# Turning x and y in pairs by VectorE's 32x32 blocks and block transfers, with wider FFN tiles, in an attention-and-FP4-FFN kernel

## The chip, the core and the metric

The kernel runs on one core of a Trainium2 chip. The metric is the device time of one execution in microseconds (us). Its engines are named as in the profile: PE is TensorE's matrix multiply and PEld its weight load, DVE is VectorE, ACT is ScalarE, POOL is GpSimd, and SP is the engine that issues most transfers (DMA).

## What is computed

The input x is 8 sequences of 1024 rows of 512 numbers, all float32. First comes attention with low-rank projections, then a feed-forward network (FFN) whose inputs and weights are rounded to a 4-bit floating-point grid; each has a layer norm before it and a residual sum after it.

```python
x = x + attn(layernorm(x))     # c_q = x@W_DQ, c_kv = x@W_DKV; 16 heads of 32 + 16 rotary;
                               # scores clipped to +-80, causal softmax, @V, @W_O
x = x + ffn(layernorm(x))

def fp4_linear(x, w): return quant(x) @ quant(w).T
def ffn(y): return fp4_linear(silu(fp4_linear(y, w_gate)) * fp4_linear(y, w_up), w_down)
# quant: blocks of 16 along the last axis; scale = max|.|/6; round to 0, .5, 1, 1.5, 2, 3, 4, 6
```

W_DQ and W_DKV are 512x128, the FFN's inner width is 1408 (11 chunks of 128).

## The kernel before

The 8192 rows are cut into 16 units of 512 rows (two per sequence), each of 4 tiles of 128 rows; two tiles are a pair, so there are 32 pairs. A matmul sums over the partitions of both operands, so the normed rows of x and the quantized rows of y (the input of FFN) must stand with their 512 columns on partitions. Both are turned by TensorE: four 128x128 transposes against an identity per tile into a PSUM bank, which ACT copies out. For x this is `turn` (L182 to L188), called by `rows_turned` (L361), and the result is the tile xnT. For y it is `turned` (L753 to L765), and the result is yT, two tiles of 512 columns per pair.

**Order of the work.** The streams of PE, DVE and ACT are written out by the program in the order of its calls. SP's transfers are placed by a scheduler, and each waits for what it needs; a place in the queue is not passed. Attention over a unit (`attention`, L667) goes step by step through 4 groups of heads and 3 or 7 key blocks; between its steps it runs `fillers`: pieces of the next unit's projection (`project_pieces`, L342), merged by their costs with pieces of FFN (`ffn_pieces`, L854) of rows that are already projected. In units 0 to 3 the pieces of the weights' preparation (`weight_pieces`, L270) stand where FFN's stand later. A small planner, `Clock`, holds expected times of PE, DVE and ACT. DVE work that is not due (all of `quantize` and the norms of y) waits in a list and is laid into DVE's stream where the planner expects room (`fill`), or at the latest where a piece asks for it by key (`need`).

**A unit's projection**: load of tiles xl, `norms`, `rows_turned`, then `rotation` (matmuls pr with wkr, pp with wdkv) and `rotated` (pp with wdq, pf), each for half a unit (one pair).

**FFN of pair m**: `fetch` loads y from mid in DRAM; `begin` lays norm and quantize; `turned`; `gate` (L786) and `up` (L805) for k = 0 to 5 run `hidden`, 16 matmuls (8 for k = 5) of 256 columns into a bank pg; ACT copies pg into h and takes its silu; DVE multiplies with the second pg (L813). Every two h tiles are quantized together, their blocks turned by DVE before and after (L214), in passes of 512 columns. `down` (L825) sums 11 chunks into pd, and `finish` adds the residual. The tiles yT, h and the raw weights share the pool `ring`: 9 places of 512 columns.

**Output projection**: at the third step of the next unit's attention `fetch_wo` (L707) loads W_O, 1 MB, into a place of the pool pT as soon as one is free, and `out_proj` (L711) runs four groups of matmuls po, adds x (reloaded as xo) and stores mid.

Of the kernel before, what the change touches and what calls it, by code (L numbers as in the profile page):

```python
# [42 lines left out]
def tile_mla_then_fp4_ffn(  # L43
# [23 lines left out]
    ring = ctx.enter_context(tc.tile_pool(name="ring", bufs=9))  # L67
# [42 lines left out]
    def mm(dst, par=1, **kw):  # L110
        shape = kw.get("tile_position", ()) and "rows" or dst.shape[0]
        clk.pe += 0.00168 * dst.shape[-1] / par + (0.1 if shape != clk.shape else 0.0)
        clk.shape = shape
        nc.tensor.matmul(dst, **kw)  # L114
# [19 lines left out]
    ones = const.tile([P, DH], F32, name="ones")  # L134
    nc.vector.memset(ones, 1.0)
    neg_half = const.tile([P, 1], F32, name="neg_half")
# [27 lines left out]
    xls = {(0, t): load_x(0, t, p2, ("xl", "y")[t // 2]) for t in range(NT)}  # L164
# [26 lines left out]
    def quantize(parts, key, turned=False):  # L191

        ends, at = [], 0
        for part in parts:
            ends.append((at, at + part.shape[1] // BLK))
            at = ends[-1][1]
        nb = at
        got = {}

        def amax(k):  # L200
            if k == 0:
                got["sc"] = p1.tile([P, 88], F32, tag="sc", name="sc")[:, :nb]
                got["rs"] = p1.tile([P, 88], F32, tag="rs", name="rs")[:, :nb]
            nc.vector.tensor_reduce(
                got["rs"][:, slice(*ends[k])],
                parts[k].rearrange("p (b k) -> p b k", k=BLK),
                AX.X,
                ALU.max,
                apply_absolute_value=True,
            )  # L210

        def turn_blocks(part):
            slack(
                0.06 + 0.0013 * part.shape[1], lambda: nc.vector.transpose(part, part), key  # L214
            )
# [11 lines left out]
        for k, part in enumerate(parts):  # L227
            if turned:
                turn_blocks(part)
            slack(0.06 + 0.0012 * part.shape[1], lambda k=k: amax(k), key)  # L230
        slack(1.1 + 0.008 * nb, scales, key)
        for part, end in zip(parts, ends):
            step, bl = part.shape[1], slice(*end)
            nbl = step // BLK
            part3 = part.rearrange("p (b k) -> p b k", k=BLK)

            def times(which, part3=part3, bl=bl, nbl=nbl):
                by = got[which][:, bl].unsqueeze(2).to_broadcast([P, nbl, BLK])
                if which == "sc":
                    nc.vector.tensor_tensor(part3, part3, by, ALU.mult)  # L240
                else:


                    nc.vector.scalar_tensor_tensor(
                        part3, part3, BELOW_ONE, by, ALU.mult, ALU.mult
                    )

            def steps(part=part, step=step):  # L250
                got["m"] = m = p1.tile([P, 512], F32, tag="m", name="m")[:, :step]
                nc.vector.tensor_scalar(
                    m.bitcast(U32), part.bitcast(U32), EXP_MASK, None, ALU.bitwise_and
                )
                nc.vector.tensor_scalar(m, m, 1.0, MAGIC, ALU.max, ALU.mult)

            def to_grid(op, part=part):
                nc.vector.tensor_tensor(part, part, got["m"], op)  # L258

            pass_cost = 0.06 + 0.00125 * step  # L260
            slack(pass_cost, lambda f=times: f("rs"), key)
            slack(1.2 * pass_cost, steps, key)
            slack(pass_cost, lambda f=to_grid: f(ALU.add), key)
            slack(pass_cost, lambda f=to_grid: f(ALU.subtract), key)
            slack(pass_cost, lambda f=times: f("sc"), key)
            if turned:
                turn_blocks(part)


    def weight_pieces():  # L270
# [10 lines left out]
        def load(i):  # L281

            raws[i] = []
            for src, _ in chunks[i]:
                for off in range(0, src.shape[1], 512):
                    width = min(512, src.shape[1] - off)
                    raw = ring.tile([P, 512], F32, tag="h", name="wraw")[:, :width]
                    nc.sync.dma_start(out=raw, in_=src[:, off : off + width])
                    raws[i].append(raw)
            quantize(raws[i], ("w", i))  # L290

        def piece(i, k, dst, off, n):
            clk.need(("w", i))
            turn(raws[i][k], dst[:, off : off + n], n)
            if k == len(raws[i]) - 1:
                raws.pop(i)
                if i + 3 < len(chunks):
                    load(i + 3)

        pieces = []  # L300
        for i, parts in enumerate(chunks):
            if len(parts) > 1:
# [5 lines left out]
        begun = [(0.5, lambda i=i: load(i)) for i in range(3)]  # L308
        return begun + [(0.5, lambda x=x: piece(*x)) for x in pieces]


    def normed(xt, key):
        got = {}

        def stats():
            pool, tag = (small, "nx") if key[0] == "x" else (p1, "ny")
            own = pool.tile([P, 10], F32, tag=tag, name=tag)
            st, ve = own[:, 0:6], own[:, 8:9]
            got["mv"], got["rstd"] = mv, rstd = own[:, 6:8], own[:, 9:10]
# [22 lines left out]
    def project_pieces(u):  # L342
# [3 lines left out]
        def fetch(*ts):  # L346
            for t in ts:
                if (u, t) not in xls:
                    xls[u, t] = load_x(u, t, p2, "xl")

        def norms(k, *ts):

            for t in ts:
                if k == 0:
                    state["norm", t] = normed(xls[u, t], ("x", u, t))
                cost, run, _ = state["norm", t][k]
                clk.dve += cost
                run()
                state["ready", t] = clk.dve

        def rows_turned(t):  # L361
            g, k = divmod(t, 2)
            if k == 0:
                state["xnT"] = p1.tile([P, NDC, 256], F32, tag="xnT", name=f"xnT_{u}_{g}")
            normed_at = state["ready", t]
            clk.pe = max(clk.pe, normed_at)
            turn(xls.pop((u, t)), state["xnT"][:, :, k * P : (k + 1) * P], NDC)

        def latent(g, w, dst):
            cols = slice(g * 256, (g + 1) * 256)  # L370
            pp = bank("pp")
            for i in range(NDC):
                mm(
                    pp[:, :256],
                    lhsT=w[:, i, :],
                    rhs=state["xnT"][:, i, :],
# [5 lines left out]
        def rotation(g):  # L382
            if g == 0:
# [3 lines left out]
                )  # L387
            pr = bank("pr")
            for i in range(NDC):
                mm(  # L390
                    pr[32 * i : 32 * i + 32, :256],
                    par=4,
                    lhsT=wkr[:, i, :],
                    rhs=state["xnT"][:, i, :],
# [29 lines left out]

        if u == 0:
# [3 lines left out]
            first, second = [], []  # L429
        else:  # L430
            first = [
                (1.0, lambda: fetch(0, 1)),
                (1.5, lambda: norms(0, 0, 1)),
                (3.0, lambda: norms(1, 0, 1)),
            ]
            second = [lambda k=k: norms(k, 2, 3) for k in range(2)]
        return [
            *first,
            (0.5, lambda: rows_turned(0)),
            (0.5, lambda: both(lambda: rows_turned(1), *[lambda: fetch(2, 3)] * (u > 0))),  # L440
            (2.3, lambda: both(lambda: rotation(0), *second[:1])),
            (2.2, lambda: both(lambda: rotated(0), *second[1:])),
            (2.0, lambda: None),
            (0.5, lambda: rows_turned(2)),
            (0.5, lambda: rows_turned(3)),
# [299 lines left out]
    def fetch(n):  # L745
        ys[n] = p2.tile([P, D], F32, tag="y", name=f"y_{n}")
        nc.sync.dma_start(out=ys[n], in_=mids[tiles[n]])

    def begin(n):
        begin_norms([(ys[n], ("y", n))])  # L750
        quantize([ys[n]], ("y", n))

    def turned(n):  # L753
        m, t = divmod(n, 2)
        clk.need(("y", n))
        if t == 0:
            yTs[m] = [ring.tile([P, 2, 256], F32, tag="h", name="yT") for _ in range(2)]
        pt = bank("pt").rearrange("p (n k) -> p n k", k=P)
        for i in range(NDC):
            nc.tensor.transpose(pt[:, i, :], ys[n][:, i * P : (i + 1) * P], ident)  # L760
            clk.pe += 0.11
        ys.pop(n)
        for i in range(2):
            to = yTs[m][i][:, :, t * P : (t + 1) * P]
            on_act(0.38, lambda: nc.scalar.copy(to, pt[:, 2 * i : 2 * i + 2, :]))  # L765

    def hidden(m, w, k):

        n = min(2, NFC - 2 * k)
        pg = bank("pg").rearrange("p (n k) -> p n k", k=256)[:, :n]  # L770
        for c in range(n):
            f0 = (2 * k + c) * P
            for i in range(NDC):
                mm(
                    pg[:, c, :],
                    lhsT=w[:, i, f0 : f0 + P],
                    rhs=yTs[m][i // 2][:, i % 2, :],
# [7 lines left out]

    def gate(m, k):  # L786
        pg = hidden(m, wg_T, k)
        if k == 0:
            hs[m] = []
        if k < NS - 1:  # L790
            h = ring.tile([P, 2, 256], F32, tag="h", name="h")
        else:
            h = p1.tile([P, 1, 256], F32, tag="h_last", name="h")
        hs[m].append(h)
        copy_out(h, pg)
        if k % 2 == 1:

            def silu(hk=hs[m][k - 1 :]):
                for h in hk:
                    on_act(0.2 + 0.0009 * h.free_size(), lambda: nc.scalar.activation(h, h, AF.Silu))  # L800
                clk.act += 2.6

            silus.append(silu)

    def up(m, k):  # L805
        while silus:
            silus.popleft()()
        h = hs[m][k]
# [227 lines left out]
```

## Time and profile before

| | |
|---|---|
| median of 3 runs | 3609.12 us (3609.05 to 3610.31) |
| profiled execution: its own time | 3609.08 us |
| its span in the trace | 3607.3 us |
| mean granted TensorE clock | 0.995 |
| moved by DMA | 131.50 MB, mean 36 GB/s |

A line of the groups reads: source line, engine, operation, written tile <- read tiles, shapes, count | busy us in all, mean ns of one | idle us of the engine just before them, and what ended it. All matmuls go through one helper, so they all have its line, L114, and are told apart by their tiles. A window's row gives the stretch, then the busy time of PE, PEld, DVE, ACT and POOL with their counts, the granted clock, DMA's busy share and GB/s. A line of the chain in order of time gives start, duration and what ran. In a timeline a row gives start, duration, engine, line and operation.

### The profile page before, as it was taken

The page shows a single profiled execution, that of the slowest core. Times are in us where ns is not written, and L with a number is a line of the kernel's source. Part 1 is how long each engine was busy: PE and PEld are TensorE (multiplying, and loading weights), DVE is VectorE, ACT ScalarE, POOL GpSimd, SP SyncE. Part 2 cuts the span into 40 slices and gives each one's busy share as a digit, 9 for nine tenths or more (in the row PEclk, how much of TensorE's full clock was granted, in tenths as well). Part 3 has the DMA queues.
Part 4 walks back from the last instruction along what each step waited for, and adds up shares of the span by engine and source line. Part 5 has one row for each costly group of instructions (what it writes and reads, how often), then busy time and mean ns, then how long its engine had stood idle before and what let it go on. Part 6 is the DMA issues. An engine that isn't in the chain of part 4 may idle for free.

```text
span 3607.3 us, 50032 instructions
## 1 busy us (share of the span) xinstructions
PE 3532.1 (98%) x19908; PEld 2038.8 (57%) x19908; DVE 2995.6 (83%) x5504; ACT 1265.2 (35%) x1778; POOL 670.1 (19%) x838
## 2 busy tenths in 40 slices
PE   8999899999999999999999999999999999999999
PEld 4334346656556566556666565655556555655576
DVE  6877858879988888888889888898878887879897
ACT  4443343333333333333333332333333332333311
POOL 3332231111111111211112111111111111112100
PEclk9999999999999999999999999999999999999999
DMA  3112101110010100011000101000110001010100
GB/s 95 62 39 72 34 13 53 45 33 24 18 58 19 53 24 24 30 47 47 24 24 19 59 21 53 21 24 33 45 47 24 24 12 59 18 47 15 50 30 15
DMA packets 77190, 131.50 MB, mean 36 GB/s; under 512 B 13852, under 2 KB 15388, under 8 KB 76956
## 3 DMA queue, kind: packets, MB, share of 16 engines
q1 hardware_dynamic: 75108, 127.43, 11.0%
q8 instruction: 157, 2.57, 0.3%
q10 hardware_dynamic: 1848, 0.87, 0.1%
q14 instruction: 77, 0.63, 0.1%
HBM read 94.72 MB, written 33.55 MB: 36 GB/s over the span
## 4 chain that ended last, share of the span: by engine, by line
PE 75%; DVE 8%; ACT 2%; issue 1%; POOL 0%; DMA 0%; ACTq 0%; POOLq 0%; DVEq 0%; SPq 0%
PE pg L114 32%; PE pd L114 13%; PE sc_ps L114 11%; PE num L114 5%; PE po L114 5%; PE pp L114 2%; PE den L114 1%; PE pk L114 1%; PE pqr L114 1%; PE pv L114 1%; PE pq L114 1%; DVE h L258 1%; ACT pT L555 1%; DVE pT L599 1%; DVE h L214 1%
## 5 line engine op out<-in xcount | busy, mean ns | idle before, releaser
L555 ACT ACTIVATE pT<-sc_ps 128x1024 f32<-128x1024 f32 (+1 forms) x640 | 566.3, 937 | 1119.2 <-PE sc_ps L114 987.0
L114 PE MATMUL pg<-yT,wu_T 128*128 128x256 f32 x2816 | 641.4, 381 | 3.5 <-ACT kT L127 1.4
L114 PE MATMUL pg<-yT,wg_T 128*128 128x256 f32 x2816 | 638.1, 382 | 1.6 <-ACT yT L765 1.0
L114 PE MATMUL pd<-wd_T,h 128*128 128x512 f32 x1408 | 618.9, 595 | 3.5 <-DVE h L214 3.5
L114 PEld LDWEIGHTS pg<-yT,wg_T 128*128 128x128 f32 x2816 | 528.1, 190 | 124.7 <-issue 39.5
L114 PEld LDWEIGHTS pg<-yT,wu_T 128*128 128x128 f32 x2816 | 526.3, 190 | 121.3 <-issue 39.9
L573 POOL TENSOR_SCALAR pT<-pT 128x1024 f32<-128x1024 f32 (+1 forms) x320 | 340.0, 1062 | 992.5 <-ACT pT L555 673.0
L577 POOL TENSOR_SCALAR_AFFINE_SELECT pT<-pT 128x256 f32<-128x256 f32 (+1 forms) x384 | 247.0, 643 | 1231.9 <-DVE pT L570 1021.6
L599 DVE TENSOR_TENSOR pT<-pT 128x1024 f32<-128x1024 f32 (+3 forms) x528 | 469.0, 912 | 6.2 <-POOL pT L577 2.8
L114 PEld LDWEIGHTS pd<-wd_T,h 128*128 128x128 f32 x1408 | 264.4, 190 | 343.0 <-issue 321.2
L570 DVE TENSOR_SCALAR pT<-pT 128x1024 f32<-128x1024 f32 (+1 forms) x320 | 207.8, 649 | 221.4 <-ACT pT L555 220.5
L114 PE MATMUL sc_ps<-qc,kT 32*128 32x512 f32 (+3 forms) x3072 | 341.0, 528 | 6.2 <-ACT pT L555 6.1
L127 ACT COPY h<-pg 128x512 f32<-128x512 f32 x192 | 105.8, 551 | 680.5 <-PE pg L114 680.5
L114 PE MATMUL num<-pT,v 128*32 128x512 f32 (+3 forms) x3072 | 321.4, 497 | 3.1 <-POOL pT L577 2.6
L114 PE MATMUL sc_ps<-qr,kr 32*128 32x512 f32 (+3 forms) x3072 | 307.2, 484 | 0.6 <-DVE qr L491 0.5
L258 DVE TENSOR_TENSOR h<-h,m 128x512 f32<-128x512 f32 (+1 forms) x384 | 263.0, 685 | 11.1
L214 DVE STREAM_TRANSPOSE h<-h 128x512 f32<-128x512 f32 (+1 forms) x384 | 250.6, 658 | 4.8
L114 PE MATMUL po<-wo,aT 128*128 128x512 f32 x512 | 229.4, 607 | 20.4 <-DMA wo<-in_w_o_dram 17.1
L114 PEld LDWEIGHTS sc_ps<-qc,kT 32*128 32x128 f32 x3072 | 114.9, 184 | 179.1 <-issue 118.6
L813 DVE TENSOR_TENSOR h<-pg,h 128x512 f32<-128x512 f32 x192 | 122.2, 638 | 110.1 <-PE pg L114 105.7
L114 PEld LDWEIGHTS sc_ps<-qr,kr 32*128 32x128 f32 x3072 | 145.4, 186 | 106.9 <-issue 82.2
L114 PEld LDWEIGHTS num<-pT,v 128*32 128x32 f32 x3072 | 66.4, 108 | 210.4 <-issue 147.8
(92 smaller groups left out, 3558.1 us busy)
## 6 DMA issues: line engine op xcount, KB each, us to landing
xo<-in_x_dram SPq DMA_DIRECT2D x64, 256.0 KB, 2.6
wo<-in_w_o_dram SPq DMA_DIRECT2D x16, 1024.0 KB, 5.1
mid<-xo SPq DMA_DIRECT2D x64, 256.0 KB, 2.1
y<-mid SPq DMA_DIRECT2D x64, 256.0 KB, 2.6
xr<-mid SPq DMA_DIRECT2D x64, 256.0 KB, 2.6
out_dram<-xr SPq DMA_DIRECT2D x64, 256.0 KB, 2.0
xl<-in_x_dram SPq DMA_DIRECT2D x62, 256.0 KB, 2.7
wraw<-in_w_gate_dram SPq DMA_DIRECT2D x11, 256.0 KB, 3.0
```

Of the source, the lines that this page charges most:

```text
L114: nc.tensor.matmul(dst, **kw)
L127: on_act(0.1 + 0.0009 * src.free_size(), lambda: nc.scalar.copy(dst, src))
L214: 0.06 + 0.0013 * part.shape[1], lambda: nc.vector.transpose(part, part), key
L258: nc.vector.tensor_tensor(part, part, got["m"], op)
L555: lambda: nc.scalar.activation(part, sc[:, 2 * k : 2 * k + 2, :cols], AF.Exp, scale=SM_SCALE),
L570: lambda: nc.vector.tensor_scalar(part, part, E_HI, E_LO, ALU.min, ALU.max),
L573: nc.gpsimd.tensor_scalar(part, part, E_HI, E_LO, ALU.min, ALU.max)
L577: nc.gpsimd.affine_select(out=diag, in_=diag, pattern=[[0, 2], [0, len(segs)], [1, P]], compare_op=ALU.is_ge, fill=0.0, base=0, channel_mu ...
L599: lambda a=whole, b=part: nc.vector.tensor_tensor(a, a, b, ALU.add),
L813: lambda: nc.vector.tensor_tensor(h, pg, h, ALU.mult),
```

## The change

1. **x's pairs.** A pair of x tiles is one tile xp of 2 x 512 columns, of which there is one place. For all units but 0, 1 and 3, DVE turns each normed tile inside its 32x32 blocks, and `settle` moves the blocks to their places in xnT by 16 transfers; the matmuls pr and pp wait for them. Units 0, 1 and 3 keep TensorE's transposes.
2. **y's pairs.** Two y tiles are loaded into one tile of 1024 columns, normed, quantized together, turned inside their blocks, and moved by 16 transfers (`moved`) into one yT tile. TensorE's transposes of y and ACT's copies are gone. `moved(m + 1)` stands after `up(m, 2)`; before, `turned` stood after `gate(m, 5)` and `up(m, 4)`.
3. **FFN's ring** has 5 places of 1024 columns: one yT, or four chunks of h. `quantize` takes one tile and runs maximum, both scalings and the turns over its full width (1024, or 768 for the last three chunks); only the rounding steps still go by 512. One silu covers a whole h tile.
4. **Operands.** The moving operands of `hidden`, `rotation` and `latent` are read as two runs of 128 columns, one for each tile of the pair. The weights `ones` are one column read 32 times.
5. **Weights.** Raw gate and up rows share one place, a raw row of w_down takes two; at most three chunks and five places are loaded ahead. The pieces are spread over units 0 to 3 as 3, 14, 21, 35 of 35 (before 5, 16, 20, 37 of 37).

```diff
-    ring = ctx.enter_context(tc.tile_pool(name="ring", bufs=9))
+    ring = ctx.enter_context(tc.tile_pool(name="ring", bufs=5))
...
-    ones = const.tile([P, DH], F32, name="ones")
-    nc.vector.memset(ones, 1.0)
+    nc.vector.memset(one_each, 1.0)
+    ones = one_each.to_broadcast([P, DH])
...
+                if k == 1 and not by_pe:
+                    clk.dve += 0.72
+                    nc.vector.transpose(xls[t], xls[t])
...
+        def settle(g):
+            state["xnT"] = xnT = p1.tile([P, 2 * NDC, P], F32, tag="xnT", name=f"xnT_{u}_{g}")
+            src = state["xp"].rearrange("p t (i q k) -> p (t i) q k", q=4, k=32)
+            for a in range(4):
+                for q in range(4):
+                    nc.sync.dma_start(
+                        out=xnT[32 * q : 32 * q + 32, :, 32 * a : 32 * a + 32],
+                        in_=src[32 * a : 32 * a + 32, :, q, :],
+                    )
+            state["there"] = max(clk.pe, clk.dve) + 13.0
...
+            (1.0, lambda: fetch(0)),
+            (1.5, lambda: norms(0, 0, 1)),
+            (1.5, lambda: norms(1, 0, 1)),
+            (5.0, lambda: settle(0)),
+            (1.0, lambda: fetch(1)),
+            (2.3, lambda: both(lambda: rotation(0), lambda: norms(0, 0, 1))),
+            (2.2, lambda: both(lambda: rotated(0), lambda: norms(1, 0, 1))),
+            (5.0, lambda: settle(1)),
+            (2.3, lambda: rotation(1)),
+            (2.2, lambda: rotated(1)),
...
-    def begin(n):
-        begin_norms([(ys[n], ("y", n))])
-        quantize([ys[n]], ("y", n))
+    def begin(m):
+        begin_norms([(ys[m][:, t, :], ("y", m)) for t in range(2)])
+        quantize(flat(ys[m]), ("y", m), turn_last=True)
...
+    def moved(m):
+        clk.need(("y", m))
+        yTs[m] = yT = ring.tile([P, 2 * NDC, P], F32, tag="h", name="yT")
+        src = ys.pop(m).rearrange("p t (i q k) -> p (t i) q k", q=4, k=32)
+        for a in range(4):
+            for q in range(4):
+                nc.sync.dma_start(
+                    out=yT[32 * q : 32 * q + 32, :, 32 * a : 32 * a + 32],
+                    in_=src[32 * a : 32 * a + 32, :, q, :],
+                )
+        arrive[m] = max(clk.pe, clk.dve) + 13.0
...
-                    rhs=yTs[m][i // 2][:, i % 2, :],
+                    rhs=yT[:, i],
...
+            yield from run(gate, 2, 3)
+            yield from run(up, 2)
             if m < last:
...
+                yield 0.0, n + 2, lambda m=m: moved(m + 1)
+            yield from run(up, 3)
+            if m + 1 < last:
+                yield 0.0, n + 4, lambda m=m: fetch(m + 2)
             yield from run(gate, 4, 5)
...
-            upto = n_weights * (5, 16, 20, 37)[u] // 37
+            upto = n_weights * (3, 14, 21, 35)[u] // 35
```

## The prediction

> **What bounds the kernel now.** I read the page first: shares, then the chain that ended last.
>
> ```profile
> PE 3532.1 (98%) x19908; PEld 2038.8 (57%) x19908; DVE 2995.6 (83%) x5504; ACT 1265.2 (35%) x1778; POOL 670.1 (19%) x838
> PE 75%; DVE 8%; ACT 2%; issue 1%; POOL 0%; DMA 0%; ACTq 0%; POOLq 0%; DVEq 0%; SPq 0%
> ```
>
> A share over the whole span can hide stages with other limits, so the windows come next (columns: stretch and its length, then the busy time of each engine).
>
> ```profile
> 0.00:540.00 540.00, 498.27 (x3822) 223.79 (x3823) 391.37 (x709) 233.08 (x333) 166.82 (x214) 0.97 0.17 53
> 540.00:1620.00 1080.00, 1074.18 (x5805) 641.58 (x5808) 925.01 (x1709) 379.65 (x532) 184.01 (x237) 1.00 0.11 36
> 1620.00:2880.00 1260.00, 1254.80 (x6781) 747.07 (x6774) 1070.92 (x1957) 448.90 (x623) 221.52 (x269) 1.00 0.10 33
> ```
>
> From 540 us on, TensorE stands still for 6 us in 1080 and for 5 us in 1260. Whatever work leaves TensorE there shortens the span, if nothing new makes it wait. Before 540 us it idles 42 us. The groups show what the change takes away, and the chain in order of time shows what that costs:
>
> ```profile
> L760 PE MATMUL pt<-ident,y 128*128 128x128 f32 x256 | 38.9, 275 | 3.4 <-DVE y L240 3.0 <-DVE h L813 0.3
> L186 PE MATMUL pt<-ident,xl 128*128 128x128 f32 x248 | 37.1, 282 | 9.1 <-DVE xl L326 6.4 <-DVE rc L657 2.1 <-ACT kT L127 0.6
> ```
>
> ```profile
> 1556.01 0.87 PE pt L186 x8
> 1568.29 0.44 PE pt L760 x4
> 1572.18 0.44 PE pt L760 x4
> ```
>
> The group's 275 ns is one transpose seen alone. In the pipeline four take 0.44 us and eight 0.87, that is 0.109 us each. The second figure is the price.
>
> **TensorE's work.** All 256 turns of y go: 256 x 0.109 = 27.9 us. Of x, units 0, 1 and 3 keep theirs; 13 units x 4 tiles x 4 = 208 go: 22.7 us. Together 50.6 us, all in a stage where TensorE is full. Nothing is added to it. FFN's and the projection's matmuls now read their 256 columns as two runs of 128. No matmul of before reads so, hence a price from nothing to, at worst, one more start-up per matmul. Eight 256-column matmuls take 1.73 us (0.216 each), which is linear with the 0.43 of 512 columns (a 13.73 us row of 32 po matmuls), so a matmul here has no visible start-up that a second run could double. I take nothing. The weights read from one column with step 0 (`ones`) are loads of 109 ns beside matmuls; nothing.
>
> **Waits that go with it.** The groups' idle times: y 3.4 us; x 9.1, of which 6.4 is the kernel's start and stays; the krope matmuls `pr` 5.9, mostly for ACT's copy of xnT, in 26 of 32 places. About 8 us.
>
> **VectorE.** It gets 52 turns of x tiles (0.70 us by L214's 512-wide row: +36 us) and 32 of y pairs. A 1024-wide pass costs less than two of 512: L599's sum takes 1236 ns against 719, so a merge saves 0.2 us. A y pair merges three passes (0.6) and six scale instructions (1.52 us at 32 blocks twice, against 1.85 at 64: 1.2 saved), and gains one turn of 1.2: -0.6 x 32 = -19 us. An h group merges five passes: 1 us x 96 groups, some -90. Sum about -75 of 2996 us: VectorE isn't made the bound. Its single passes grow from 0.7 to 1.2 us, and a pass that frees a bank for TensorE stands in order behind them. Today the 5632 pg matmuls idle 5 us in all for such reasons, so I take 4 us more, bounds 0 and 10. ACT loses the copies L765 (41.6 us) and 52 of L188 (31 us), at 35% hidden anyway: nothing.
>
> **The transfers.** 58 pairs x 16 = 928 block transfers on SP, each 32 partitions x 8 runs of 128 bytes = 256 packets. The nearest rows are the only 128-byte transfers of before, at the start: 2048 packets each.
>
> ```profile
> 6.18 4.09 SPq L174 DMA_DIRECT2D wqc<-in_w_q_dram  x1
> 10.32 3.16 SPq L175 DMA_DIRECT2D wqr<-in_w_q_dram  x1
> ```
>
> 256/2048 of that is 0.40 to 0.51 us per transfer; the issue of any transfer takes 0.33. So 16 take 6.4 to 8.2 us, and the last lands about 2.1 later (mid<-xo): 8.5 to 10.3. I take 10. The order view of the changed kernel shows each transfer waiting for the semaphore of the one issued eight earlier, so eight fly together. If they didn't overlap at all: 16 x (2.1 + 0.4) = 40 us. Those are the ends.
>
> What covers it? Along the order of the changed kernel I counted TensorE's work (rates as above) between the last result that VectorE and SP's queue need before the last block transfer may go, and the first matmul that reads the moved pair, less VectorE's own passes after that result. The shortest of the 58 covers are 15.5 and 16.2 us (the two last y pairs, where no attention lies between), then three of 19.7; 49 are over 27.9, the median is 36.8. At 10 us no pair comes late: 0. At 20 us the covers' shortfall sums to 9 us, at 28 us to 53, at 34 us to 151, at 40 us to 321.
>
> Here a rule speaks against the change. The Trainium skill ("VectorE: DVE Perf Modes", The three transpose paths) warns that a plain copy which transposes by its access pattern is 19 times slower than one through the transposing hardware when the innermost destination step is large. If moving a pair (512 KB; 256 KB land in 2.1 us here, so 4.2) took 19 times as long, 80 us, the shortfall over all 58 covers would be 2,210 us. By the row above it is none. I go with the row: VectorE has already turned inside the 32x32 blocks, so what moves is a run of 32 elements, the 128 bytes of that row, and not single elements.
>
> **SP's queue.** The block transfers wait for VectorE at the head of SP's queue, and xo, mid, out and wo stand behind. SP's issues rise by 928 x 0.45 = 420 us of 3607, no bound by itself. The one load that TensorE meets at once is wo:
>
> ```profile
> wo<-in_w_o_dram SPq DMA_DIRECT2D x16, 1024.0 KB, 5.1
> ```
> ```profile
> 1527.02 3.72 PE L114 MATMUL pg<-yT,wg_T 128*128 128x256 f32 x16
> 1527.18 0.38 SPq L709 DMA_DIRECT2D wo<-in_w_o_dram  x1
> 1530.58 3.62 PE L114 MATMUL pg<-yT,wu_T 128*128 128x256 f32 x16
> 1534.03 13.90 PE L114 MATMUL po<-wo,aT 128*128 128x512 f32 x32
> ```
>
> It is issued when its place comes free, lands 5.1 us later, and two FFN steps (6.9 us) cover that by 1.7. In the changed order five of the 16 wo loads have one step (3.4 us) where they had two, so TensorE would wait 1.7 us; and in the same five units eight block transfers (3.6 us) are queued ahead of wo, which can add up to 2. Five waits of 1.7 to 3.7: 9 to 19 us; I take 12, added to the 20 us that po waits today.
>
> Weights, units 0 to 3: two fewer loads ahead, pieces spread 3, 14, 21, 35. The turns of raw weights idle 13 us today; this may grow or shrink by 8. I take 0. The wide ring is as tight as before (a pair holds 4 of 5 tiles where it held 7 of 9, and reuse waits for the same matmuls): 0.
>
> **Sum**, against the profiled execution (span 3607.3 in 3609.08 us): 3607.3 - 50.6 - 8 + 4 + 12 = 3564.7, and with the 1.8 us around the span 3566.5; say 3567. The median shown, 3609.12, is the same run's time within 0.1.
>
> **Rivals.**
> 1. SP's queue jams more than counted. For it: five wo loads stand behind half a burst, and mids stand between block transfers. Against: TensorE runs behind SP elsewhere. Price: half of the 16 wo loads behind a whole burst (7.2 us), less what they have to spare, some 5.4 each: 43 us in place of my 12, so 3598.
> 2. The gain is made up by small waits everywhere (late banks, the weights' stage at its worst, the jam): -58.6 + 43 + 10 + 8 gives 3612, no difference.
> 3. Slower: the block transfers come late. One mechanism, in front of the first gate or `pr` matmul of a pair. It decides from about 27 us per pair (1.5 us per transfer, as if fewer than two overlapped): there the shortfall passes the net gain of 42.6. At 34 us: +151, 3718. Against it: 0.4 to 0.5 us in the nearest row. For it: that row reads from HBM, spread over 128 partitions; here 32 partitions write 32.
>
> **Chances.** Forecast 0.66; jam 0.15; better than 3546 through a shorter weights' stage 0.02; no change 0.06; slower 0.11. A measurement can tell about 0.2% (7 us), so faster by more 0.83, within 0.06, slower 0.11. The forecast's own range: 3567 - 20 (no wo wait, weights -8) to 3567 + 21 (wo 19, weights +8, passes 10). To hold 8 in 10 it must take in most of the jam: 3546 to 3604.
>
> **What would show it.** TensorE's busy time near 3481, `pt` groups of y gone and of x down to 48; first gate and `pr` matmuls with no idle before them on DMA; yT's 16 issues within about 8 us; po's idle near 32 us; VectorE near 2920. I am wrong if the pg group's pace leaves 0.216 us, if idle before pg or pr on a DMA passes 20 us, or if po's exceeds 60.

## The result and the profile after

The changed kernel takes 3774.65 us (median of 4 runs, 3772.24 to 3774.99) where the kernel before takes 3609.09 beside it: a ratio of 1.046 (interval 1.044 to 1.048). It is 165.6 us slower. The forecast was 3567, faster; the time lies outside the range, on the other side, and beyond the price of the slower rival too.

The page of the changed kernel, the busy times and the chain by engine:

```profile
PE 3540.2 (94%) x19444; PEld 2011.3 (53%) x19444; DVE 2976.9 (79%) x4804; ACT 1185.1 (31%) x1498; POOL 690.8 (18%) x838
PE 70%; DVE 12%; DMA 1%; issue 1%; ACT 1%; SPq 1%; POOL 0%; DVEq 0%; POOLq 0%; ACTq 0%
```

464 TensorE instructions are gone, and still TensorE is busy 8 us longer and idle 157 us longer. VectorE's share of the ending chain grew from 8% to 12% while its own busy time fell by 19 us. So VectorE has more room than before and yet holds TensorE up. The windows, for the two stretches that were full before:

```profile
540.00:1620.00 1080.00, 1031.40 (x5402) 605.32 (x5394) 875.75 (x1398) 339.18 (x418) 184.20 (x227) 0.98 0.16 42
1620.00:2880.00 1260.00, 1208.13 (x6380) 706.80 (x6382) 1027.16 (x1637) 400.95 (x493) 215.10 (x263) 0.98 0.17 43
```

They are no longer full: 49 and 52 us of idle where there were 6 and 5, and the granted clock, 1.00 before, is 0.98. The groups say who is waited for:

```profile
L114 PE MATMUL pd<-wd_T,h 128*128 128x512 f32 x1408 | 661.2, 625 | 96.0 <-DVE h L210 96.0
L114 PE MATMUL po<-wo,aT 128*128 128x512 f32 x512 | 243.6, 637 | 57.8 <-DMA wo<-in_w_o_dram 57.7
L197 PE MATMUL pt<-ident,wraw 128*128 128x128 f32 x132 | 23.4, 308 | 44.5 <-DVE wraw L230 27.2 <-issue 17.3
L114 PE MATMUL pr<-xnT,wkr 128*32 128x256 f32 x256 | 20.6, 394 | 1.5 <-ACT xnT L199 1.5
```

The first two in the kernel before:

```profile
L114 PE MATMUL pd<-wd_T,h 128*128 128x512 f32 x1408 | 618.9, 595 | 3.5 <-DVE h L214 3.5
L114 PE MATMUL po<-wo,aT 128*128 128x512 f32 x512 | 229.4, 607 | 20.4 <-DMA wo<-in_w_o_dram 17.1 <-DVE wraw L240 2.1 <-DVE rs L204 1.0
```

The matmuls `pd` of w_down idle 96.0 us (3.5 before), always for VectorE's last turn of a chunk of h; `po` 57.8 (20.4); the turns of raw weights 44.5 (13.2). The first readers of block transfers do not wait for them: `pr` idles 1.5 us, for ACT's copies in the units that kept TensorE's turns, and the gate matmuls 1.0, for VectorE.

**What a wait in front of pd looks like.** The timeline of TensorE in the changed kernel (start, duration, engine, operation, and in brackets the idle time and its releaser):

```profile
1447.45 3.60 PE L114 MATMUL pd<-wd_T,h 128*128 128x512 f32 x8
1454.11 5.40 PE L114 MATMUL pd<-wd_T,h 128*128 128x512 f32 x8 [3.06 <-DVE h L210]
1464.57 4.54 PE L114 MATMUL pd<-wd_T,h 128*128 128x512 f32 x6 [5.06 <-DVE h L210]
```

And that of VectorE, from some 15 us earlier:

```profile
1430.99 2.37 DVE L210 STREAM_TRANSPOSE h<-h 128x1024 f32<-128x1024 f32 x2
1435.37 0.69 DVE L620 TENSOR_SCALAR pT<-pT 128x1024 f32<-128x1024 f32 x1 [2.00 <-ACT pT L605]
1435.97 1.22 DVE L215 TENSOR_REDUCE rs<-h 128x64 f32<-128x1024 f32 x1
...
1452.81 2.10 DVE L210 STREAM_TRANSPOSE h<-h 128x1024 f32<-128x1024 f32 x2
...
1463.53 0.98 DVE L210 STREAM_TRANSPOSE h<-h 128x768 f32<-128x768 f32 x1
```

From 1448.26 to 1464.5 VectorE works with no break over 0.05 us on the quantization of the last two h groups, and TensorE waits twice for it, 8.1 us in all. But at 1433.4 VectorE stood idle 2.00 us in front of softmax's pass L620, whose input ACT had not yet made, while the pass L215, ready to run, stood behind it in the stream. In all VectorE idles 3772 - 2977 = 795 us. In this place the work was there, and was written behind a pass that could not start yet.

**What a wait in front of po looks like.** SP's timeline in the changed kernel (issues of equal transfers in a row are one line):

```profile
1076.24 5.18 SPq L389 DMA_DIRECT2D xnT<-xp  x8
1081.58 0.48 SPq L759 DMA_DIRECT2D wo<-in_w_o_dram  x1
1082.10 6.24 SPq L389 DMA_DIRECT2D xnT<-xp  x8
```

And TensorE's:

```profile
1076.93 0.85 PE L114 MATMUL num<-pT,v 128*32 128x384 f32 x8
1077.72 3.72 PE L114 MATMUL pg<-yT,wg_T 128*128 128x256 f32 x16
1087.88 4.60 PE L114 MATMUL po<-wo,aT 128*128 128x512 f32 x5 [6.44 <-DMA wo<-in_w_o_dram]
```

Eight issues take 5.18 us, 0.65 each. TensorE freed the place for W_O at 1077.8 with its last `num` matmul; the load is issued 3.8 us later, lands 6.2 us after that, and one FFN step covers 3.5: 6.5 by this sum, 6.44 in the trace.

### The profile page after: what moved, and what is told of

It reads as the page before. It is cut to its first block, busy times and chain, and to the rows that moved or that the text cites. A ratio compares the mean times of both kernels' runs of the same rounds, so it can differ in the third digit from the quotient of the medians.

```text
span 3772.1 us, 49429 instructions
## 1 busy us (share of the span) xinstructions
PE 3540.2 (94%) x19444; PEld 2011.3 (53%) x19444; DVE 2976.9 (79%) x4804; ACT 1185.1 (31%) x1498; POOL 690.8 (18%) x838
## 4 chain that ended last, share of the span: by engine, by line
PE 70%; DVE 12%; DMA 1%; issue 1%; ACT 1%; SPq 1%; POOL 0%; DVEq 0%; POOLq 0%; ACTq 0%
PE pg L114 30%; PE pd L114 12%; PE sc_ps L114 10%; PE po L114 5%; PE num L114 5%; PE pp L114 2%; DVE h L256 2%; DMA wo<-in_w_o_dram 1%; DVE h L210 1%; PE pk L114 1%; PE pqr L114 1%; PE pv L114 1%; PE pq L114 1%; PE den L114 1%; DVE pT L649 1%
## 5 line engine op out<-in xcount | busy, mean ns | idle before, releaser
L114 PE MATMUL pd<-wd_T,h 128*128 128x512 f32 x1408 | 661.2, 625 | 96.0 <-DVE h L210 96.0
L623 POOL TENSOR_SCALAR pT<-pT 128x1024 f32<-128x1024 f32 (+1 forms) x320 | 350.0, 1094 | 1057.5 <-ACT pT L605 887.3
L114 PEld LDWEIGHTS pd<-wd_T,h 128*128 128x128 f32 x1408 | 276.3, 199 | 459.2 <-issue 337.1
L649 DVE TENSOR_TENSOR pT<-pT 128x1024 f32<-128x1024 f32 (+3 forms) x528 | 479.8, 933 | 4.3 <-POOL pT L627 0.9
L620 DVE TENSOR_SCALAR pT<-pT 128x1024 f32<-128x1024 f32 (+1 forms) x320 | 208.3, 651 | 273.8 <-ACT pT L605 272.8
L114 PE MATMUL po<-wo,aT 128*128 128x512 f32 x512 | 243.6, 637 | 57.8 <-DMA wo<-in_w_o_dram 57.7
L256 DVE TENSOR_TENSOR h<-h,m 128x512 f32<-128x512 f32 (+1 forms) x384 | 263.2, 685 | 10.4
L210 DVE STREAM_TRANSPOSE h<-h 128x1024 f32<-128x1024 f32 (+2 forms) x194 | 216.3, 1131 | 2.4
L114 PEld LDWEIGHTS po<-wo,aT 128*128 128x128 f32 x512 | 104.1, 206 | 190.6 <-issue 170.9
```

The costliest lines, as they stand in the source:

```text
L210: slack(0.06 + 0.0013 * width, lambda: nc.vector.transpose(q, q), key)
L620: lambda: nc.vector.tensor_scalar(part, part, E_HI, E_LO, ALU.min, ALU.max),
L623: nc.gpsimd.tensor_scalar(part, part, E_HI, E_LO, ALU.min, ALU.max)
L649: lambda a=whole, b=part: nc.vector.tensor_tensor(a, a, b, ALU.add),
```

## The experiments

The planner's rule for VectorE's stream is in `fill` (L95 in both kernels): a piece of waiting work is laid into a gap only if `max(self.dve, q[0][3]) + q[0][0] <= until`, that is if it fits whole by the planner's costs. What doesn't fit stays in the list until `need` asks for it, all at once, in front of the matmul that waits.

**Theory A**: the change made the pieces long (1.29 us of planned cost for 1024 columns where 0.7 did for 512), so they seldom fit a gap, the backlog moves to the deadline, and TensorE waits there. The order of the stream makes the loss, not what the new operations cost. Counted in the planner, the cost that is left to `need` in front of `down` is 110 us before and 213 in the changed kernel. The rivals, which the expectations call by other letters, lay the loss on the changed operations themselves (the long passes and turns, the block transfers on SP's queue). For `po` the question is a second one: the queue, or the FFN step that no longer covers the load. Each ratio is to runs of the kernel before on the same chip (3609.09 for the changed kernel, 3611.49 for e1 to e4, 3610.36 for e7 to e10, 3609.14 for the rest).

| run | time, us | ratio to before (interval) | idle before pd / po / raw weights / num, us | PE busy, us |
|---|---|---|---|---|
| before | 3609.09 | | 3.5 / 20.4 / 13.2 / 3.1 | 3532.1 |
| changed | 3774.65 | 1.046 (1.044 to 1.048) | 96.0 / 57.8 / 44.5 / 6.4 | 3540.2 |
| e1 passes of 512 | 3638.06 | 1.007 (1.006 to 1.009) | 26.0 / 53.6 / 18.7 / 9.3 | 3498.8 |
| e2 rule + 0.6 | 3618.21 | 1.002 (1.001 to 1.003) | 0.6 / 48.6 / 16.6 / 21.6 | 3500.8 |
| e3 x by TensorE | 3744.44 | 1.037 (1.035 to 1.039) | 81.9 / 26.6 / 45.6 / 5.5 | 3544.8 |
| e4 y by TensorE | 3740.81 | 1.036 (1.034 to 1.038) | 49.1 / 50.0 / 44.5 / 8.2 | 3554.1 |
| e7 e2, wo on ACT | 3624.63 | 1.004 (1.003 to 1.006) | 0.6 / 45.7 / 16.7 / 21.9 | 3500.2 |
| e8 e2, x by TensorE | 3587.15 | 0.994 (0.993 to 0.995) | 0.6 / 21.0 / 12.8 / 11.7 | 3505.4 |
| e9 before, rule + 0.6 | 3610.37 | 1.000 (1.000 to 1.001) | 0.1 / 18.9 / 0.3 / 13.8 | 3533.4 |
| e10 rule + 0.3, wo on ACT | 3611.14 | 1.001 (1.000 to 1.002) | 4.2 / 45.6 / 16.7 / 16.9 | 3497.0 |
| e11 before, rule - 0.6 | 4353.78 | 1.206 (1.204 to 1.208) | 234.8 / 28.5 / 43.0 / 5.0 | 3699.9 |
| e12 rule + 0.3, x by TensorE | 3579.54 | 0.992 (0.990 to 0.993) | 6.1 / 24.5 / 10.6 / 3.1 | 3503.8 |
| e14 e2, settle earlier | 3570.61 | 0.989 (0.988 to 0.991) | 0.6 / 33.6 / 3.3 / 26.0 | 3481.8 |
| e15 rule + 0.3, settle earlier | 3573.55 | 0.990 (0.988 to 0.991) | 0.9 / 35.3 / 6.7 / 20.3 | 3483.1 |

**e1: the passes cut to 512 columns again**, in the changed kernel.

```diff
+        cuts = [(o, min(o + 512, width)) for o in range(0, width, 512)]
-        slack(pass_cost(width), amax, key)
+        for o, e in cuts:
...
+            slack(pass_cost(e - o), lambda o=o, e=e: amax(o, e), key)
```

Both scalings and the turns likewise.

> The changed kernel with the passes of the quantization cut to 512 columns again (turns, maximum, both scalings), all else as changed. Theory A (TensorE waits in front of pd because wide passes rarely fit the gaps that the planner sees, so h's last passes are laid only where pd's piece asks for them): the work forced at that point, counted along the program's own order, is 110 us before, 213 in the changed kernel and 166 here, so pd's idle falls from 96 us to about 50, the wraw turns' from 45 to about 30, and the time to about 3680. Theory B (VectorE simply has too much to do between due points; width helps it): pd's idle stays at 90 or above and the time is 3770 to 3800. Theory C (the block transfers jam SP's queue): no change within 15 us of 3774.

Measured 3638.06 us, 136.6 less than the changed kernel, though VectorE has more instructions (5452 for 4804) and is busy 74 us longer. pd's idle falls to 26.0 us, the raw weights' to 18.7. More came back than was expected. By itself this can't tell A from a rival that dislikes long passes; e2 can.

**e2: the same instructions, another rule of laying.** What differs is the order of VectorE's stream. In the traces VectorE runs the same 4804 instructions in both, ACT's order is the same, TensorE's too but for a few num and den matmuls in the weights' stage, and on POOL only the small steps of the norms move along.

```diff
-                    if q and max(self.dve, q[0][3]) + q[0][0] <= until and q[0][3] <= self.dve:
+                    if q and max(self.dve, q[0][3]) + q[0][0] <= until + 0.6 and q[0][3] <= self.dve:
```

> The changed kernel with one term in the planner's fill: a pass may overrun the gap that it is laid into by 0.6 us. The passes are as wide and as many as in the changed kernel; only their order in VectorE's stream differs. Theory A: work forced in front of pd falls from 213 to 29 us, so pd's idle falls below 15 us, the clock recovers, and the time is 3590 to 3640. Theory B: the same work has no more room, the wait moves to the h<-pg products or to num, and the time stays within 30 us of 3774. Theory C: no change within 15 us.

Measured 3618.21 us, 156.4 less. The groups of this run:

```profile
L114 PE MATMUL pd<-wd_T,h 128*128 128x512 f32 x1408 | 620.6, 597 | 0.6 <-DVE h L210 0.6
L114 PE MATMUL num<-pT,v 128*32 128x512 f32 (+3 forms) x3072 | 329.4, 498 | 21.6 <-POOL pT L627 20.1 <-DVE pT L620 1.4
L114 PE MATMUL po<-wo,aT 128*128 128x512 f32 x512 | 240.3, 630 | 48.6 <-DMA wo<-in_w_o_dram 48.6
```

The 96 us before pd are gone with every 1024-wide pass, every turn and every block transfer still in place. The rivals for this part of the loss fell here. A price shows as well: a pass that hangs over its gap holds up softmax's passes behind it, and `num` idles 21.6 us (6.4). po's wait stays.

**e3 and e4: one half undone each.** e3 turns all of x by TensorE, e4 turns y by TensorE; the rule stays as it was.

```diff
-        by_pe = u in (0, 1, 3)
+        by_pe = True
```
```diff
-        quantize(flat(ys[m]), ("y", m), turn_last=True)
+        quantize(flat(ys[m]), ("y", m))
...
+        for t in range(2):
+            turn(rows[:, t, :], yT[:, t * NDC : (t + 1) * NDC, :], NDC)
```

> The changed kernel with x turned by TensorE in all units (no turns of x on VectorE, no block transfers of x, 22.7 us of TensorE's work back); y as changed. Theory A: forced work 196 us for 213, pd's idle about 80; po's idle falls from 58 to about 25, as the load of wo no longer stands behind VectorE's turns; time about 3720. Theory B: the x turns are what overfills VectorE, pd's idle falls below 30 and the time below 3680. Theory C: half of the block transfers are gone, and pd's idle and po's both halve.

> The changed kernel with y turned by TensorE at the place where the transfers stood (no turns of y pairs on VectorE, no block transfers of y, 27.9 us of TensorE's work back); x and the wide passes as changed. Theory A: forced work 167 us for 213, pd's idle about 50; po's idle stays near 58; time about 3730. Theory B: pd's idle barely moves, 85 or more, since y's turn is only 38 us of VectorE's work; time near 3790. Theory C: half of the block transfers are gone, and pd's idle and po's both halve.

Measured 3744.44 and 3740.81 us, both somewhat slower than expected. Neither half alone makes the loss: with x's block transfers gone pd still idles 81.9 us, with y's turns and transfers gone 49.1. Only po answers to one of them: 26.6 us without x's transfers, 50.0 without y's.

**e7 and e10: W_O's load taken off SP's queue.** In e7 ACT issues it, with the rule of e2; e10 is the same with 0.3 in place of 0.6.

```diff
-        nc.sync.dma_start(out=outs["wo"], in_=w_o.rearrange("(c p) n -> p c n", p=P))
+        nc.scalar.dma_start(out=outs["wo"], in_=w_o.rearrange("(c p) n -> p c n", p=P))
```

> The kernel with the 0.6 us overrun, and W_O's load issued from ACT's queue instead of SP's; nothing else differs. Theory A2 (in the five units whose wo stands behind eight block transfers, SP issues it 4 us after its place is free, and it then shares the queues with eight more): po's idle falls from 49 us to 20 to 28, the clock recovers a little, and the time is 3575 to 3590. Theory D (wo's place itself comes free too late, because VectorE's turns of x stand ahead of the clip and the sums): po's idle stays above 40 and the time within 8 us of 3618.

> As the kernel with wo on ACT's queue, with an overrun of 0.3 instead of 0.6 us. Work forced in front of pd is 58 us for 29 (changed kernel: 213). Theory A: pd's idle stays below 8; num's idle, 22 us with 0.6 as the clip stands behind overrunning passes, falls to about 12; time within 10 us of the run with 0.6, on either side.

Measured 3624.63 and 3611.14 us. e7 missed: po still idles 45.7 us where 20 to 28 were expected. The waits of the five units that lost a step shrank together from 30.5 us (e2) to 21.2, but ACT's own queue delays the issue by up to 3 us, and three other waits of 3 us came up. So the queue seems not to be the larger cause of po's wait; e14 decides. e10 is 13.5 us below e7 by the medians, where under 10 were expected; num idles 16.9 us instead of 21.9, where 12 were expected.

**e8: e2 with x by TensorE.**

> The kernel with the 0.6 us overrun, and x turned by TensorE in all units. Theory A2: the five bursts ahead of wo are gone and two of FFN's steps stand between again, so po's idle falls from 49 to about 25; pd's stays below 5; 22.7 us of TensorE's work come back: 3618 - 24 - 8 + 23 = 3609, 3600 to 3615. Theory D expects the same of this run: it is here for the price of x's part alone, the difference to the run with wo on ACT's queue.

Measured 3587.15 us, faster than the kernel before, and better than expected. Against e2 it gives 22.7 us of turns back to TensorE and is still 31 us faster: po idles 21.0 us (48.6), num 11.7 (21.6). As ordered, x's half costs more than it brings.

**e9: the kernel before with the rule of e2.**

> The kernel before, with the same 0.6 us overrun in the planner's fill. Theory A: with passes of 512 columns the planner's gaps were wide enough (work forced in front of pd 110 us, pd's idle 3.5), so there is little to win: 3600 to 3615. A rival (the overrun is simply a better plan for any version, so its gain says nothing of the wide passes): at least 30 us faster, below 3580.

Measured 3610.37 us, no difference: before, pd had 3.5 us to lose. So e2's gain is not one that the loose rule gives to any kernel.

**e11: the kernel before with a tighter rule.** The same line with `until - 0.6`: none of the change's operations is in it, only the shortage of fitting gaps.

> The kernel before with one change to its planner: a piece of VectorE's waiting work is laid only where the gap has 0.6 us more room than the piece needs. No block transfer, no pass of 1024 columns, no TensorE work is changed. In the program's order the waiting work that is left to the last moment grows: in front of the down matmuls from 110 to 322 us, of the upper chunks of h from 5 to 202, of the turns of y from 1 to 261. Theory A (the order of VectorE's stream, not the change's own operations, made the changed kernel slow): pd's idle time rises from 3.5 us to 60 or more, the turns of y wait too, and the time rises to 3690 to 3900 us. Rival (VectorE catches up by itself because it has room; wide passes or block transfers are needed to make TensorE wait): within 10 us of 3610.

Measured 4353.78 us, far above what A expected, and with A's signature:

```profile
L114 PE MATMUL pd<-wd_T,h 128*128 128x512 f32 x1408 | 718.2, 663 | 234.8 <-DVE h L214 234.8
L760 PE MATMUL pt<-ident,y 128*128 128x128 f32 x256 | 51.9, 339 | 310.2 <-DVE y L240 310.2
```

A piece of 0.7 us that must find 1.3 us of room is placed as a piece of 1.3 us is. This alone makes a kernel with 512-wide passes and TensorE's turns 745 us slower. The rule here tightens for every piece, also for the rounding steps that the change left at 512, so it overdoes the change's own effect; the counts in the planner tell the direction, not the microseconds (e1 and e4, with counts of 166 and 167, idle 26.0 and 49.1 us before pd).

**e12: x by TensorE, the rule at + 0.3.**

> The changed kernel with all of x turned by TensorE, and the planner's gap rule loosened by 0.3 us in place of the 0.6 of the run that took 3587 us. Theory A, with its second half (a pass that hangs over its gap delays softmax's num, 11.7 us of idle there): num's idle falls to 6 to 9 us, pd's stays under 6, time 3578 to 3588. Rival (0.3 leaves too much to the last moment): pd's idle above 15 us and a time of 3592 or more.

Measured 3579.54 us, within A's range. pd's idle is 6.1, at the edge of the 6 expected; num's fell further than expected, to 3.1.

**e14 and e15: the lost FFN step put back.** In the changed kernel with the loose rule (0.6 and 0.3), the assumed cost of one piece is cut, which lets the merge place it a step earlier:

```diff
-            (5.0, lambda: settle(0)),
+            (3.0, lambda: settle(0)),
```

By the order of the program, all five units with one FFN step between W_O's place and po have two again; every block transfer is kept, on SP's queue. The merge moves other pieces along with this one, so TensorE's order differs from e2 in more places than these.

> The changed kernel with the gap rule loosened by 0.6 us, and the assumed cost of the first settle piece cut from 5.0 to 3.0, which sets that piece earlier among FFN's pieces: all five units that had one FFN step (3.4 us) between wo's release and po have two again (6.9). Nothing else is changed beside the run at 3618 us: all block transfers stay, on the same queue. Theory S (the lost step is what makes po wait): po's idle falls from 48.6 us to 20 to 30, half-clock time from 96 to about 65, time 3580 to 3598. Theory Q (the block transfers in SP's queue, ahead of wo and beside its landing, make it wait): po's idle stays above 38, time 3608 to 3620.

> As the run with the first settle piece at a cost of 3.0, but with the gap rule loosened by 0.3 us in place of 0.6. Under theory A with its second half (hanging passes delay num: 21.6 us idle at 0.6, 16.9 at 0.3): 5 to 12 us less than that run, pd's idle under 8. Rival: no difference (within 4 us).

Measured 3570.61 and 3573.55 us: the best of all, about 1% faster than the kernel before (ratio 0.989, interval 0.988 to 0.991, for e14). The page and groups of e14:

```profile
PE 3481.8 (98%) x19444; PEld 1994.9 (56%) x19444; DVE 2946.3 (83%) x4804; ACT 1184.7 (33%) x1498; POOL 701.9 (20%) x838
```
```profile
L114 PE MATMUL num<-pT,v 128*32 128x512 f32 (+3 forms) x3072 | 326.4, 497 | 26.0 <-POOL pT L627 24.8 <-DVE pT L620 1.2
L114 PE MATMUL po<-wo,aT 128*128 128x512 f32 x512 | 233.9, 616 | 33.6 <-DMA wo<-in_w_o_dram 33.6
```

TensorE runs the changed kernel's 19444 matmuls in 3481.8 us, and pd idles 0.6. One of the five places, in the timelines of SP and TensorE:

```profile
1016.57 4.51 SPq L389 DMA_DIRECT2D xnT<-xp  x7
1021.25 0.48 SPq L759 DMA_DIRECT2D wo<-in_w_o_dram  x1
```
```profile
1018.11 3.72 PE L114 MATMUL pg<-yT,wg_T 128*128 128x256 f32 x16
1021.66 3.62 PE L114 MATMUL pg<-yT,wu_T 128*128 128x256 f32 x16
1027.32 4.96 PE L114 MATMUL po<-wo,aT 128*128 128x512 f32 x11 [2.04 <-DMA wo<-in_w_o_dram]
```

The load is issued 3.1 us after its place is free, as late as in e2 (3.1 there), but a second step stands in front of po, and the wait is 2.04 us instead of 5.36. Over the five units: 30.5 us in e2, 12.1 here. Of the wait in these units 18 us belong to the lost step, and about 12 remain with the queue and the longer landing. po's 33.6 us are a little above the 20 to 30 expected. The time is 9 us below its range: the raw weights' wait fell too (16.6 to 3.3), and so did TensorE's busy time (3500.8 to 3481.8). So of the 47.6 us between e2 and e14 only po's part is traced to the lost step. For e15 the rival held: between 0.6 and 0.3 there is no difference here; what num gains, the raw weights and po lose.

## Why the prediction was wrong

The sum's terms, against the trace of the changed kernel (idle times before the group):

| term | predicted | measured | off by, us |
|---|---|---|---|
| TensorE's busy time | 3532.1 - 50.6 = 3481.5 | 3540.2 | +58.7 |
| pd, for VectorE's order | 3.5 (not priced) | 96.0 | +92.5 |
| turns of raw weights | 13.2 (+- 8) | 44.5 | +31.3 |
| po, for W_O | 20.4 + 12 = 32.4 | 57.8 | +25.4 |
| turns of x and y, pr | 18.4 - 8 = 10.4 | 8.5 | -1.9 |
| num, sc_ps, pg, for longer passes | 15.0 + 4 = 19.0 | 19.6 | +0.6 |

The errors sum to 206.6 us: 3564.7 + 206.6 = 3771.3, against a span of 3772.1.

**The step that failed** is the one on VectorE: "VectorE isn't made the bound", and "a pass that frees a bank for TensorE stands in order behind them. [...] I take 4 us more". I asked how much work VectorE has and how long one pass blocks the next, and for both the answer holds: num, sc_ps and pg idle 4.6 us more than before. I did not ask where the program would write the passes, and put pd at nothing more. Line 95 stands in the code: a piece is laid if it fits whole. Pieces of nearly twice the length against gaps as they were change the whole order, and e2 shows that the order is worth 156 us. The length alone makes 70 of pd's 92.5 us (e1); which of the other moves spoil the order for the rest no run tells apart. The order explains pd, most of the raw weights' excess (16.6 us in e2 where 44.5), and through the gaps the clock below. VectorE's saving of 75 us was too high as well: 18.7 measured, 49 in e2 and e14.

**TensorE's busy time** was right as an amount of work and wrong as a time. With fewer long gaps between (6 over 2.3 us for 37), e14 needs 3481.8 us for the same matmuls, within 0.3 of the 3481.5 predicted, and in the changed kernel 16 gate matmuls take 3.72 us as before, so the operands of two runs of 128 cost nothing that can be seen, as I took it. In the changed kernel the granted clock drops after gaps. The windows around the two gaps above (the column of three digits such as 0.84, after POOL, is the clock):

```profile
1447.50:1454.00 6.50, 3.55 (x9) 1.28 (x7) 6.14 (x9) 0.00 (x0) 1.66 (x3) 1.00 0.00 0
1454.10:1464.50 10.40, 5.40 (x8) 2.03 (x8) 9.78 (x19) 0.00 (x0) 0.00 (x0) 0.84 0.00 0
1464.60:1469.10 4.50, 4.50 (x10) 1.68 (x10) 0.00 (x0) 0.00 (x0) 0.00 (x0) 0.62 0.00 0
```

Eight pd matmuls take 3.60 us before the first gap and 5.40 after it. Summed from the clock records within the span, the changed kernel runs 211.6 us at half clock, the kernel before 37.5. An extra of 174.1 us at half clock goes with 58.7 us of extra busy time, 0.34 us per us; in e4, e3 and e2, counted against their own matmuls, it is 0.37, 0.31 and 0.35. The Trainium skill ("TensorE: Matmul & The Clock Gate", HAM oscillation) states this: a pause in TensorE's work over a window of 3.4 us gives half the clock afterwards, at a cost of half the throttled time. The trace agrees in kind: half clock comes in stretches of 3.4 us and multiples. In size it differs twice. Gaps of 2.3 to 3.3 us were already followed by it in 6 cases of 10 (all 27 longer ones were). And the cost was 0.34, not 0.5, for TensorE is busy in only 142.0 of the 211.6 us at half clock (before, 25.2 of 37.5): half of the busy time alone, (142.0 - 25.2) / 2, is 58.4 us. I did not price this at all. That the gaps cause it is the page's reading; no run set the clock alone. And e14 doesn't fit to the microsecond: with 38.7 busy us at half clock this sum asks for 6.8 us more than 3481.5, and it shows 0.3, so part of that match is luck.

**W_O's load**: the mechanism was foreseen, one step lost in five units and block transfers ahead; the size was off. I gave the queue "up to 2" us from issues of 0.45 us. They take 0.65 in a row, W_O goes out 3.8 us late in the place shown, and lands in 5.7 us (median) instead of 5.1, beside the transfers that follow it. The sum then gives 6.5 us for that place, where I had 1.7 to 3.7. Over the five units the waits are 34.8 us, where I had 9 to 19.

**What held.** The turns left and nothing came in their place. The block transfers:

```profile
L811 SPq DMA_DIRECT2D yT<-y x512: 585/609/1605, 513.9 to 3674.9; - x171
DMA to landing us min/median/max: 1.9/2.0/5.1
```

An issue takes 609 ns and a transfer lands after 2.0 us (median). The 16 issues of a pair of y take 10.9 us from first to last (median, 10.4 at the least) where I had 8, so with the last landing 13 against the 10 taken, still under the shortest counted cover of 15.5. No pair comes late. The row was the better guide than the warning of 19 times, which would have made 80 us of a pair, and rival 3, which needed 27 us, is out: the loss has its sign but not its mechanism. None of the signs that I had named as fatal appeared (the pace of the gate matmuls is 381 ns in the groups, as before; pg and pr hardly wait; po stays under 60): they watched the operands, the block transfers and W_O's load, and the loss was in pd. Rival 1's jam is there in part (po).

With the order mended and the step put back (e14), the change gives 3570.61 us, 3.6 from the forecast. That it comes so near is in part luck: num, sc_ps and pg idle 35.9 us there (19.0 in the sum), which the raw weights with 3.3 (13.2) and pd with 0.6 (3.5) make up for. The working priced a kernel that the program's planner did not write.

## What to carry to other kernels

When a program lays work into gaps of a plan, the length of a piece is a scheduling parameter: before merging two passes, ask what fits the gaps afterwards, not only what the merge saves. Look for idle time of the engine that is waited for; if it idles and is late, its order is the first suspect, and a run with the same instructions in another order settles it. Every load that TensorE meets at once has a cover that can be counted in steps; here losing a step cost more (18 us) than the queue of short transfers with the longer landing (12 us). Price a gap on TensorE with the slow clock that followed it here.

## What the hardware showed that was not expected

- With 33 of the 37 gaps over 2.3 us between TensorE's matmuls in the changed kernel came half clock for 3.4 to 13.7 us, starting within the gap or up to 1.4 us behind it. With it go 58.7 us of busy time, on top of 157 us of added idle.
- A block transfer of 256 runs of 128 bytes holds SP's queue for 0.61 us (median) and 0.65 in a row, against 0.38 for 1 MB of W_O. Its landing, 2.0 us for 32 KB, is that of the quickest transfers of 256 KB (2.0 to 2.9 by kind).
- The load of W_O lands in 5.7 us (median) where it took 5.1 before and 5.3 in e14; with eight block transfers issued right behind it, in the place shown, it took 6.2. No run measured this by itself.
